# A four-layer kernel on one core: the order of its first loads, edge coefficients spread by TensorE, and buffer waits tile by tile

## The chip, the cores and the metric

The kernel runs on one core of a Trainium2 chip. A core has five engines that work side by side, each with its own stream of instructions taken strictly in order: TensorE (PE in the profile; PEld is its loading of weights), VectorE (DVE), ScalarE (ACT), GpSimd (POOL) and SyncE (SP), which here only issues transfers. ScalarE and GpSimd issue transfers too; 16 DMA engines carry all of them. The metric is device time in microseconds (us) of one launch; the median of several launches counts.

## The reference, cut to what matters

The input x has 8 sequences ("batches") of 512 rows and 512 columns, all float32. Four layers follow one another.

```python
# L0: one step of a grid operator, per batch, with finite differences
df = -(grad(A0*f, rows) + grad(A1*f, cols)) + 0.5*(grad2(B0*f, rows) + grad2(B1*f, cols) + 2 mixed terms of B2*f)
x = maximum(f + df*dt[b], 0)            # one-sided formulas on the first and last row and column
# L1: adaLN, 16-head attention with a bias and a mask, residual, then an MLP
emb = silu(sin_emb(tok)) @ W_ada + b_ada;  scale, shift = split(emb)
x = ln(x)*(1+scale) + shift
x = x + softmax(q @ k.T / sqrt(32) + bias, masked) @ v @ Wo + bo     # q, k, v = x @ Wq + bq, ...
x = x + gelu(( ln(x)*g2 + beta2 ) @ W1 + b1) @ W2 + b2
# L2: one expert per batch (Wi[e], Wo[e]), residual, layer norm
# L3: a low-rank response added with a gated strength (uses sigmoid(safety[b]))
```

In L0 the interior of the grid is the same formula everywhere; the first and the last row ("edge rows") have formulas of their own. The coefficients A and B are shared by all batches, so their combinations are formed once.

## The kernel before, in words

The program is one long list for each engine. The order on an engine is written out by hand: `pin` (`tc.keep_in_program_order`) holds an instruction at its place in the list. There are three stages.

`grid_stage` (the front) works on batch 0. It loads A and B (tiles a0, a1, b0, b1, b2), forms the coefficient sums ca, cb, cc, ce, cg on VectorE, multiplies each with f (batch 0 of x) into e, g, c, ga, gb, q, t, and lets TensorE add them up in four PSUM tiles `acc` (the profile's l_0 to l_3, one for each row that a partition holds) by multiplying with shifted identity matrices `zi`. On the way it stores the sums to DRAM as `coef_q`, `coef_e`, `coef_c`, `coef_g`, `coef_a`, `coef_b` (from GpSimd's queue, after `gate_c`), where the other batches read them again.

The edge rows of all 8 batches are computed together in a packed layout: 64 partitions stand for 4 column blocks x 2 sides x 8 batches. `fe` holds the values and `ec` the twelve rows of coefficients; `ec` is the same for all batches, so before the change `edge_in` fills it with eight broadcast loads of 8 partitions each, one after another on GpSimd's queue behind `gate_e`, a small instruction that waits for f. The result `xe` is stored to DRAM (`xed`) for the later batches, and its rows of batch 0 are copied into x (`x<-xe`, two transfers on SP, two on ACT). Then come the layer norm's statistics (`stats`), the normalisation, and `embed` (64 small matmuls, tile `pe`) with `embed_out` (tile `ada`), which give scale and shift.

`attention_stage` runs over units: batch, group of 4 heads, block of 128 rows; 128 units. Batch 0 is turned with 16 transposes (`xtr`), made into x1 by `x1_in`, and multiplied into q and k (`q_block`, `k_block`). Each unit loads two bias tiles `bt`, adds the mask on GpSimd (`add_mask`), and runs scores, softmax, transposes and values. In the same stage VectorE does the grid of the next batch in steps (`grid_early`, `grid_step`): it loads f with its neighbour rows (`gf`) and one coefficient half after another (`gq`, `x<-coef_e`, `gc`, `gg`, `ga`, `gb`), in the order that the table `GRID` gives. Step 0 is two products with gq, step 1 the product with coef_e, step 2 a difference, the product with gc, and the ghosts of the columns.

`mlp_stage` runs 16 passes: 8 of the MLP and 8 of the experts, with a seven-product form of the matmuls, whose operands are sums of quarters (`w_quads`, `b_quads`).

Tiles come from pools. A pool is opened for a stage and closed at its end, and the next pools take its memory. Transfers of SP and ACT take eight completion semaphores in turn, in program order over both; a transfer waits until the one that had its semaphore before has landed. GpSimd's have eight of their own.

In the built program the first loads stand so on SP's list (semaphore waits in brackets by their number): b1 half, a1 half, b1 half [1], a1 half [3], b0 [4], a0 [7], f [0], b2 [1], W_ada halves, Wq, Wk, Wv, Wo, bq, bk, bv, bo, then eight value loads of expert numbers, then the edge rows, mask and gf. ScalarE's list begins with ten small loads (tok, freq, b_ada, safety, eidx, ghost weights, dt, g2, beta2, b1). The first load of attention on SP (the mask `mu`) waits for all transfers, GpSimd's included, that used the memory of the closed pools.

Lines that the steps below touch: 104 to 111 (small loads), 168 (`load_w`), 175 to 178 (rows), 243 (grid matmuls), 274 to 289 (loads of the front), 386 to 393 (coef stores), 479 (xed), 492 (edge rows), 499 (stats), 546 and 543 (transposes and matmuls of attention), 588 (x1), 663 (grid sums), 973 (the softmax's first step), 1137 and 1143 (matmuls and sums of the MLP).

Of the kernel before, what the change touches and what calls it, by code (L numbers as in the profile page):

```python
# [11 lines left out]
F32 = mybir.dt.float32  # L12
# [3 lines left out]
AF = mybir.ActivationFunctionType  # L16
# [23 lines left out]
def fused_kernel(ctx: ExitStack, tc: tile.TileContext, a: dict):  # L40
# [65 lines left out]
    nc.scalar.dma_start(freq, a["c_freq"])  # L106
    bada = ep.tile([P, 2 * KC], F32, name="bada")
    nc.scalar.dma_start(bada, a["b_ada"])
    nc.scalar.dma_start(sigs, a["safety"][None, :].to_broadcast([P, NB]))
    nc.scalar.dma_start(eidx, a["eidx"][None, :])  # L110
    nc.vector.tensor_scalar(bada[:, 0:KC], bada[:, 0:KC], 1.0, None, ALU.add)
# [27 lines left out]
    nc.scalar.activation(sigs, sigs, AF.Sigmoid)  # L139
# [14 lines left out]

    def embed_out(pe):
        tc.keep_in_program_order(
            nc.vector.tensor_tensor(
                ada, pe, bada[:, :, None].to_broadcast([P, 2 * KC, NB]), ALU.add
            )
        )  # L160
# [4 lines left out]
    def load_w():  # L165
        for n in ("Wq", "Wk", "Wv", "Wo"):
            w[n] = w8(wo8, n)
            nc.sync.dma_start(w[n], a[n].rearrange("(k p) m -> p k m", p=P))
# [5 lines left out]
    def load_rows():  # L174
        nc.sync.dma_start(bqk[:, 0, :], a["bq"])
        nc.sync.dma_start(bqk[:, 1, :], a["bk"])
        nc.sync.dma_start(bvc, a["bv"].rearrange("(k p) -> p k", p=P))
        nc.sync.dma_start(bo, a["bo"][None, :].to_broadcast([P, D]))
# [3 lines left out]
        embed_out,  # L182
# [3 lines left out]
    io = ctx.enter_context(tc.tile_pool(name="io", bufs=1))  # L186
    g2 = const.tile([P, 2, KC], F32, name="g2")
    nc.scalar.dma_start(g2[:, 0, :], a["g2"])
    nc.scalar.dma_start(g2[:, 1, :], a["beta2"])
    b1 = const.tile([P, NJ], F32, name="b1")  # L190
    nc.scalar.dma_start(b1, a["b1"])
# [4 lines left out]
        g2, mhalf,  # L196
# [18 lines left out]
def grid_stage(  # L215
    tc, a, const, small, dram, x, mhalf, ident, load_wada, load_w, load_rows, embed,
    embed_out,
# [27 lines left out]
    with ExitStack() as ctx:  # L245
# [22 lines left out]
        pin(nc.gpsimd.memset(ec, 0.0))  # L268
# [7 lines left out]
        with tc.tile_pool(name="raw", bufs=1) as rp:  # L276
# [4 lines left out]
            def edge_in(i, k):  # L281
                lo, hi = max(0, W * k - 1), min(D, W * k + W + 1)
                u = slice(lo - W * k + 1, hi - W * k + 1)
                p0 = n * i
                pin(nc.gpsimd.dma_start(fe[p0 : p0 + n, :, u], a["edge_f"][:, :, lo:hi]))
                for side in range(2):
                    p1 = p0 + side * NB
                    pin(
                        nc.gpsimd.dma_start(
                            ec[p1 : p1 + NB, :, u],  # L290
                            a["edge_c"][side : side + 1, :, lo:hi].to_broadcast([NB, 12, hi - lo]),
                        )
                    )
# [9 lines left out]
            nc.scalar.dma_start(gw, a["c_ghost"].to_broadcast([P, 16]))  # L303
            nc.scalar.dma_start(dth, a["dt"][None, :].to_broadcast([P, NB]))
            load_wada()
            load_w()
# [6 lines left out]
            for i, k in enumerate(blocks):  # L313
                edge_in(i, k)
# [11 lines left out]
        wp = ctx.enter_context(tc.tile_pool(name="l0", bufs=1))  # L326
# [54 lines left out]
        for m, w, o in (  # L381
            ("q", b2, 1), ("e", ce, 1), ("c", cc, 0), ("g", cg, 1), ("a", ca, 0), ("b", cb, 0)
# [94 lines left out]
        xed = dram.tile([n, D], F32, name="xed")  # L477
        for i, k in enumerate(blocks):
            pin(nc.gpsimd.dma_start(xed[:, W * k : W * k + W], xe[n * i : n * i + n, :]))
        pe = embed(ps)  # L480
        pin(nc.vector.tensor_scalar(dth, dth, 0.5, None, ALU.mult))
        st = small.tile([P, R, 6], F32, name="ln0_st", tag="ln0_st", bufs=1)
        mv = small.tile([P, R, 2], F32, name="ln0_mv", tag="ln0_mv", bufs=1)
        for r in (0, 3, 1, 2):
            stt(x[:, r, :], acc[r], dth[:, 0:1], f[:, r, :], ALU.mult, ALU.add)
            pin(nc.scalar.activation(x[:, r, :], x[:, r, :], AF.Relu))
        for o, u, c in ((0, 3 * n, 0), (n, n, 2 * W)):
            for side, q_ in ((0, nc.sync), (1, nc.scalar)):
                p, r = side * (P - 1), side * (R - 1)
                e0 = o + side * NB  # L490
                pin(
                    q_.dma_start(
                        x[p : p + 1, r, c : c + 2 * W].rearrange("o (b w) -> o b w", w=W),
                        xe[e0 : e0 + u + 1 : u, :],
                    )
                )
# [24 lines left out]
def attention_stage(  # L521
    tc, a, small, xp, xt, x_home, x1d, grid, ident, sc1, shift, io, wo8, w, rows,
    g2, mhalf,
# [11 lines left out]
    with ExitStack() as ctx:  # L535
        wp = ctx.enter_context(tc.tile_pool(name="aw", bufs=1))
        pp = ctx.enter_context(tc.tile_pool(name="ap", bufs=2))
        ps = ctx.enter_context(tc.tile_pool(name="a_ps", bufs=1, space=PSUM))
# [508 lines left out]
        load_bias(*units[0])  # L1047
        grid_loads(1, -1)
        mask_in(0, 1)
        load_bias(*units[1])  # L1050
        for c in range(KC):
            x1_in(0, c)
        mask_out(0, 0)
# [3 lines left out]
        grid_early(0)  # L1057
# [5 lines left out]
        mask_in(0, 3)  # L1063
        grid_early(2)
# [44 lines left out]
def mlp_stage(tc, a, small, xp, io, wo8, x1d, ident, eidx, sigs, layernorm, rstd_of, phalf, wl3, g2, b1, first):  # L1109
# [19 lines left out]
    with ExitStack() as ctx:  # L1129
        wp = ctx.enter_context(tc.tile_pool(name="fw", bufs=1))  # L1130
        ap = ctx.enter_context(tc.tile_pool(name="fa", bufs=2))
        ps = ctx.enter_context(tc.tile_pool(name="f_ps", bufs=2, space=PSUM))
# [725 lines left out]
```

## Time and profile before

| | us |
|---|---|
| median of 3 runs | 2807.26 (2805.81 to 2810.29) |
| the profiled execution | 2809.32 |
| its span (first to last instruction) | 2807.5 |
| front and start, to the first softmax of unit 0 | 88.1 |
| attention, to the first matmul of the MLP | 88.1 to 1143.3 |
| MLP and experts | 1143.3 to the end |

| engine | busy us | share of the span |
|---|---|---|
| TensorE | 2729.1 | 97% |
| VectorE | 1942.0 | 69% |
| GpSimd | 1503.9 | 54% |
| ScalarE | 1002.8 | 36% |

A row of a profile names a line of the kernel, an engine, an operation and a tile (out<-in). "Busy" is the time in which the engine had an instruction. A bracket after a timeline row is the time for which the engine was idle before it and what ended that; SPq, ACTq and POOLq rows are issues of transfers, and a long issue is one that could not be handed to its queue. The chain of waits is followed back from the last instruction, at each step to what released it.

### The profile page before, as it was taken

The page shows a single profiled execution, that of the slowest core. Times are in us where ns is not written, and L with a number is a line of the kernel's source. Part 1 is how long each engine was busy: PE and PEld are TensorE (multiplying, and loading weights), DVE is VectorE, ACT ScalarE, POOL GpSimd, SP SyncE. Part 2 cuts the span into 40 slices and gives each one's busy share as a digit, 9 for nine tenths or more (in the row PEclk, how much of TensorE's full clock was granted, in tenths as well). Part 3 has the DMA queues.
Part 4 walks back from the last instruction along what each step waited for, and adds up shares of the span by engine and source line. Part 5 has one row for each costly group of instructions (what it writes and reads, how often), then busy time and mean ns, then how long its engine had stood idle before and what let it go on. Part 6 is the DMA issues. An engine that isn't in the chain of part 4 may idle for free.

```text
span 2807.5 us, 39790 instructions
## 1 busy us (share of the span) xinstructions
PE 2729.1 (97%) x14654; PEld 2011.6 (72%) x14654; DVE 1942.0 (69%) x3581; ACT 1002.8 (36%) x2133; POOL 1503.9 (54%) x1081
## 2 busy tenths in 40 slices
PE   5999999999999998999999999999999999999998
PEld 3455555555555554788888888888888888888886
DVE  6888898988888766576666756655466556556554
ACT  1466666666666666212111211211121121121221
POOL 3455555555555654466566655656456545535633
PEclk9999999999999999999999999999999999999998
DMA  9665657566666554542533444253223133143120
GB/s 300 225 204 180 235 172 241 186 223 214 194 233 191 157 160 158 181 121 49 158 124 83 109 143 124 49 169 120 73 97 125 59 137 128 42 154 113 42 75 31
DMA packets 190400, 405.62 MB, mean 144 GB/s; under 512 B 24104, under 2 KB 28784, under 8 KB 183934
## 3 DMA queue, kind: packets, MB, share of 16 engines
q1 hardware_dynamic: 185192, 391.93, 42.2%
q0 software_dynamic: 3680, 11.07, 3.2%
q8 instruction: 117, 1.92, 0.3%
q14 instruction: 77, 0.63, 0.1%
q10 hardware_dynamic: 1334, 0.07, 0.0%
HBM read 367.32 MB, written 31.50 MB: 142 GB/s over the span
## 4 chain that ended last, share of the span: by engine, by line
PE 86%; DVE 9%; ACT 2%; DMA 2%; issue 1%; SPq 0%; DVEq 0%; ACTq 0%; POOL 0%
PE y L1137 28%; PE u L1137 28%; PE tr L546 6%; PE s L543 4%; PE ctx L543 4%; PE o L543 3%; PE pv L543 3%; PE pq L543 3%; PE pk L543 2%; DVE bt L973 2%; DVE x L663 2%; DVE pt L998 1%; DMA Wo<-in_Wo 1%; ACT bt L978 1%; PE po L1137 1%; PE btr L1140 1%
## 5 line engine op out<-in xcount | busy, mean ns | idle before, releaser
L1137 PE MATMUL y<-wo,act 128*128 128x256 f32 x2560 | 578.9, 381 | 0.0
L950 POOL TENSOR_TENSOR bt<-bt,mk 128x1024 f32<-128x1024 f32 x256 | 543.2, 2142 | 64.2 <-DMA bt<-in_bias 61.2
L1137 PEld LDWEIGHTS y<-wo,act 128*128 128x128 f32 x2560 | 479.4, 190 | 82.2 <-issue 20.6
L978 ACT ACTIVATE bt<-bt,mn 128x512 f32<-128x512 f32 x512 | 365.4, 715 | 115.5 <-DVE mn L973 115.4
L546 PEld LDWEIGHTS tr<-ident,bt 128*128 128x128 f32 x2048 | 228.2, 141 | 167.7 <-issue 115.7
L1137 PE MATMUL u<-bt,wi 128*128 128x256 f32 x1440 | 330.5, 379 | 0.0
L973 DVE CUSTOM_DVE_ANT_0 bt<-s,bt 128x512 f32<-128x512 f32 x512 | 330.4, 682 | 0.0
L1143 DVE TENSOR_TENSOR act<-u,u 128x512 f32<-128x512 f32 x256 | 173.3, 686 | 209.9 <-PE u L1137 132.6
L1137 PEld LDWEIGHTS u<-bt,wi 128*128 128x128 f32 x1440 | 273.5, 190 | 37.2
L546 PE MATMUL tr<-ident,bt 128*128 128x128 f32 x2048 | 279.9, 278 | 18.8 <-DVE pt L998 7.7
L998 DVE COPY pt<-tr 128x512 f32<-128x512 f32 x256 | 175.8, 687 | 113.3 <-PE tr L546 113.0
L1137 PE MATMUL u<-tb,ws 128*128 128x256 f32 x1024 | 242.1, 379 | 0.0
L1137 PE MATMUL y<-t,s 128*128 128x256 f32 x1024 | 234.2, 380 | 0.0
L1000 ACT COPY pt<-tr 128x512 f32<-128x512 f32 x256 | 148.1, 579 | 183.1 <-PE tr L546 180.7
L1137 PEld LDWEIGHTS u<-tb,ws 128*128 128x128 f32 x1024 | 194.4, 190 | 26.5
L1146 POOL TENSOR_TENSOR t<-wo,t 128x512 f32<-128x512 f32 x64 | 104.5, 1647 | 200.5 <-PE y L1137 200.5
L1137 PEld LDWEIGHTS y<-t,s 128*128 128x128 f32 x1024 | 191.1, 190 | 24.1
L1457 ACT ACTIVATE act<-act,b 128x512 f32<-128x512 f32 x128 | 82.9, 711 | 292.4 <-DVE act L1143 292.4
L1457 ACT ACTIVATE act<-act,bi 128x512 f32<-128x512 f32 x128 | 83.8, 713 | 282.6 <-DVE act L1143 282.6
L1143 DVE TENSOR_TENSOR x<-y,x 128x512 f32<-128x512 f32 x96 | 64.5, 685 | 159.0 <-PE y L1137 105.1
L543 PE MATMUL s<-kt,qt 32*128 32x512 f32 x1024 | 171.7, 645 | 2.3 <-DVE mn L973 1.4
L1143 DVE TENSOR_TENSOR u<-u,u 128x512 f32<-128x512 f32 x192 | 131.3, 684 | 58.8 <-PE u L1137 58.8
(314 smaller groups left out, 4283.5 us busy)
## 6 DMA issues: line engine op xcount, KB each, us to landing
bt<-in_bias SPq DMA_DIRECT2D x256, 512.0 KB
wo<-in_W SPq DMA_DIRECT2D x32, 1024.0 KB
wi<-in_Wi SPq DMA_DIRECT2D x32, 1024.0 KB
wo<-in_Wo_e SPq DMA_DIRECT2D x32, 1024.0 KB
wi<-in_W SPq DMA_DIRECT2D x28, 1024.0 KB
gq<-coef_q SPq DMA_DIRECT2D x21, 512.0 KB
x1d<-x SPq DMA_DIRECT2D x8, 1024.0 KB
x<-x1d SPq DMA_DIRECT2D x8, 1024.0 KB
```

The source lines that it names most:

```text
L543: pin(nc.tensor.matmul(out, lhsT=lhsT, rhs=rhs, start=start, stop=stop))
L546: pin(nc.tensor.transpose(out, src, ident))
L663: pin(nc.vector.tensor_tensor(out, x, y, op))
L950: nc.gpsimd.tensor_tensor(bt, bt, mask[b, r][:, None, :].to_broadcast([P, 2, S]), ALU.add)
L973: nc.vector.tensor_tensor_reduce(bt[:, i, :], ss[h], bt[:, i, :], -1.0, 3.0e38, ALU.add, ALU.min, mn)
L978: nc.scalar.activation(bt[:, i, :], bt[:, i, :], AF.Exp, bias=mn, scale=-1.0, accum_out=sums[b, c, r][:, h : h + 1],)
L998: pin(nc.vector.tensor_copy(pt[:, :, r % 2, :], tr))
L1000: pin(nc.scalar.copy(pt[:, :, r % 2, :], tr))
L1137: pin(nc.tensor.matmul(out, lhsT=lhsT, rhs=rhs, start=start, stop=stop))
L1143: pin(nc.vector.tensor_tensor(out, x, y, op))
L1146: pin(nc.gpsimd.tensor_tensor(out, x, y, op))
L1457: nc.scalar.activation(acts[g][:, k, :], acts[g][:, k, :], func, bias=bi[:, j : j + 1])
```

## The change

It changes the front, the order of a few loads of attention, and how pools hand on their memory.

- Loads: safety goes first on SP, and only tok and freq stay on ScalarE. Ghost weights, dt, b_ada and eidx go on SP, behind the grids and W_ada. Wv and Wo leave the front: they are issued in attention, Wv behind the first bias and Wo behind the second. g2, beta2 and b1 go on SP, further behind (`load_late`).
- Edge coefficients: `ec8` is loaded once for 8 partitions (4 blocks x 2 sides) in four loads at the start of GpSimd's queue, and TensorE spreads each to 8 batches with a selection matrix `sel8`, in four matmuls (`pec`); ScalarE copies the four results into `ec`. Only the four loads of `fe` stay behind `gate_e`.
- The edge rows of batch 0 are issued right after rows 0 and 3 have been made, before ScalarE's Relu of rows 1 and 2. `xed` is stored from ScalarE's queue instead of GpSimd's. `coef_g` is stored before `coef_c`. The addition to b_ada stands behind the edge chain.
- `reuse_waits="tile"` on eight pools: an instruction that takes over memory of a closed pool waits for the users of the tiles that lay there, not for all of the pool. In the built program the mask's load waits for the stores of coef_a and coef_b, one of coef_q's rows, an edge row's transfer, and points on TensorE and GpSimd; gf's load for those of coef_e and coef_g and an edge row's. The first matmul of the MLP, which waited for VectorE and ScalarE, waits for ScalarE.
- Attention: `grid_early(0)` moves in front of the first mask and `q_block`, so that VectorE has the two products with gq before the first q.

```diff
+    nc.sync.dma_start(sigs, a["safety"][None, :].to_broadcast([P, NB]))
+    nc.scalar.activation(sigs, sigs, AF.Sigmoid)
     bada = ep.tile([P, 2 * KC], F32, name="bada")
-    nc.scalar.dma_start(bada, a["b_ada"])
-    nc.scalar.dma_start(sigs, a["safety"][None, :].to_broadcast([P, NB]))
-    nc.scalar.dma_start(eidx, a["eidx"][None, :])
...
     def load_rows():
+        nc.sync.dma_start(bada, a["b_ada"])
+        nc.sync.dma_start(eidx, a["eidx"][None, :])
...
-    io = ctx.enter_context(tc.tile_pool(name="io", bufs=1))
+    io = ctx.enter_context(tc.tile_pool(name="io", bufs=1, reuse_waits="tile"))
...
+    def load_late():
+        for t, v in ((g2[:, 0, :], "g2"), (g2[:, 1, :], "beta2"), (b1, "b1")):
+            tc.keep_in_program_order(nc.sync.dma_start(t, a[v]))
...
+            ec8 = rp.tile([N // NB, 12, W + 2], F32, name="ec8")
+            sel8 = rp.tile([N // NB, N // NB, NB], F32, name="sel8")
+            pin(nc.gpsimd.memset(ec8, 0.0))
...
+            for i, k in enumerate(blocks):
+                c, u = edge_cols(k)
+                pin(nc.gpsimd.dma_start(ec8[2 * i : 2 * i + 2, :, u], a["edge_c"][:, :, c]))
...
-            nc.scalar.dma_start(gw, a["c_ghost"].to_broadcast([P, 16]))
-            nc.scalar.dma_start(dth, a["dt"][None, :].to_broadcast([P, NB]))
+            nc.sync.dma_start(gw, a["c_ghost"].to_broadcast([P, 16]))
+            nc.sync.dma_start(dth, a["dt"][None, :].to_broadcast([P, NB]))
             load_wada()
-            load_w()
+            load_w("Wq", "Wk")
             load_rows()
...
             for i, k in enumerate(blocks):
-                edge_in(i, k)
+                c, u = edge_cols(k)
+                pin(nc.gpsimd.dma_start(fe[n * i : n * i + n, :, u], a["edge_f"][:, :, c]))
+
+            for i in range(4):
+                pec = ps.tile([N, 3, W + 2], F32, name=f"pec_{i}", tag="pec", bufs=2)
+                mm(
+                    pec, sel8.rearrange("q s b -> q (s b)"), ec8[:, 3 * i : 3 * i + 3, :],
+                    True, True,
+                )
+                pin(nc.scalar.copy(ec[:, 3 * i : 3 * i + 3, :], pec))
...
-            ("q", b2, 1), ("e", ce, 1), ("c", cc, 0), ("g", cg, 1), ("a", ca, 0), ("b", cb, 0)
+            ("q", b2, 1), ("e", ce, 1), ("g", cg, 1), ("c", cc, 0), ("a", ca, 0), ("b", cb, 0)
...
         for r in (0, 3, 1, 2):
             stt(x[:, r, :], acc[r], dth[:, 0:1], f[:, r, :], ALU.mult, ALU.add)
             pin(nc.scalar.activation(x[:, r, :], x[:, r, :], AF.Relu))
...
+            if r == 3:
+                edges()
+        xed = dram.tile([n, D], F32, name="xed")
+        for i, k in enumerate(blocks):
+            pin(nc.scalar.dma_start(xed[:, W * k : W * k + W], xe[n * i : n * i + n, :]))
...
-        ps = ctx.enter_context(tc.tile_pool(name="a_ps", bufs=1, space=PSUM))
+        wp = ctx.enter_context(tc.tile_pool(name="aw", bufs=1, reuse_waits="tile"))
+        pp = ctx.enter_context(tc.tile_pool(name="ap", bufs=2, reuse_waits="tile"))
+        ps = ctx.enter_context(tc.tile_pool(name="a_ps", bufs=1, space=PSUM, reuse_waits="tile"))
...
         load_bias(*units[0])
+        load_w("Wv")
         grid_loads(1, -1)
         mask_in(0, 1)
         load_bias(*units[1])
+        load_w("Wo")
         for c in range(KC):
             x1_in(0, c)
+        grid_early(0)
         mask_out(0, 0)
         pin(nc.scalar.copy(bvr, bvc[:, :, None].to_broadcast([P, KC, P])))
         add_mask(*units[0])
         drain(q_block(0, 0))
-        grid_early(0)
         grid_early(1)
         drain(k_block(0, 0, "ctx"))
         mask_out(0, 1)
         load_bias(*units[2])
         mask_in(0, 2)
         mask_in(0, 3)
+        load_late()
         grid_early(2)
```

## The prediction, made before the changed kernel was run

> **What bounds the kernel now.** I read the page first: the slices of TensorE (PE) and the shares of the chain that ended last.
>
> ```profile
> PE   5999999999999998999999999999999999999998
> ...
> PE 86%; DVE 9%; ACT 2%; DMA 2%; issue 1%; SPq 0%; DVEq 0%; ACTq 0%; POOL 0%
> ```
>
> PE carries 86% of the chain, so an edit counts only where PE has nothing to do, and the first slice (70 us, digit 5) is the one place where the page shows that. So I read the chain of waits for the first 100 us (start, duration, what).
>
> ```profile
> 26.67 34.86 DMA Wo<-in_Wo
> ...
> 61.56 3.29 DMA x<-xe
> ...
> 70.00 3.42 PE xtr L546 x16
> ```
>
> The chain runs through Wo, which lands at 61.53 and which nobody needs there: the edge rows (x<-xe) were issued behind it. The timeline of SP, of DVE and of PE shows who stands in whose way; the bracket is idle time before the row, and what ended it.
>
> ```profile
> 39.66 14.48 SPq L178 DMA_DIRECT2D bo<-in_bo  x1
> 60.72 1.38 SPq L492 DMA_DIRECT2D x<-xe  x2
> 64.93 0.34 SPq L564 DMA_DIRECT2D mu<-in_mask  x1
> 65.32 0.42 SPq L687 DMA_DIRECT2D gf<-in_x  x1
> ```
>
> ```profile
> 64.76 0.69 DVE L499 BATCH_NORM_STATS2 ln_st<-x 128x6 f32<-128x512 f32 x1 [7.64 <-DMA x<-xe]
> ...
> 76.89 0.75 DVE L617 TENSOR_SCALAR qt<-pq,bqk 128x512 f32<-128x512 f32 x1 [3.25 <-PE pq L543]
> 77.56 4.28 DVE L663 TENSOR_TENSOR gq<-gq,gf 128x1024 f32<-128x1024 f32 x2
> 81.76 3.14 DVE L663 TENSOR_TENSOR x<-x,gf 128x1024 f32<-128x1024 f32 x1
> ```
>
> ```profile
> 54.32 9.04 PE L148 MATMUL pe<-sc,wada 128*128 128x8 f32 x64
> 70.00 3.42 PE L546 MATMUL xtr<-ident,x 128*128 128x128 f32 x16 [6.64 <-DVE ada L157]
> ```
>
> SP hung on bo for 14.48 us, the edge rows came late, DVE idled 7.64 us for them, and the loads of attention (mu, gf) went out only at 65. The last view is busy time by stage (PE, PEld, DVE, ACT, POOL; then PE's clock, DMA share, GB/s).
>
> ```profile
> 6.00:12.00 6.00, 0.00 (x0) 0.00 (x0) 3.20 (x15) 3.68 (x6) 0.00 (x0) 1.00 0.70 206
> 28.00:44.00 16.00, 16.00 (x39) 7.31 (x38) 14.13 (x21) 0.17 (x1) 7.56 (x15) 1.00 1.07 215
> 44.00:62.00 18.00, 18.00 (x84) 12.23 (x82) 12.24 (x38) 2.52 (x4) 7.05 (x24) 0.93 1.03 414
> 62.00:68.00 6.00, 1.36 (x7) 1.26 (x6) 1.97 (x6) 0.00 (x0) 1.05 (x1) 0.50 0.42 116
> 72.00:88.00 16.00, 15.22 (x46) 7.18 (x45) 11.85 (x15) 5.18 (x7) 6.04 (x2) 0.97 1.03 383
> ```
>
> At 28 to 44 the DMAs are full and yet move only 215 GB/s (eight small broadcast loads of ec and four of fe run then); at 62 to 68 everything waits. From the first softmax (88.11) DVE works without a gap to 131, then PE takes over. So a shift of 88.11 passes to the end unchanged, and the sum is about that moment.
>
> **The change, part by part.**
>
> *First loads.* Before, SP's third load was issued at 5.81 and f at 10.47, because both queues take eight completion semaphores in turn and the early turns were small ScalarE loads (SP waited 4.2, 1.3 and 1.7 us for such). Now five loads go at once, and a0, f, b2 wait for tok, safety and freq, of which tok and freq landed by 6.0 and 7.4. ScalarE issued ten DMAs in the front, now two, so its table loads (1.28 us each; first at 7.67) begin earlier; the ang chain, which waited 1.52 us for the first Sin, ends about 1.2 us earlier, 9.8 for 11.02. DVE's waits in the coefficient sums (1.01, 0.38, 0.23) go, as do small gaps: from 9.8, two halves 4.6, cc 2.3, ce and cg 4.4 put e at 21.1 instead of 24.19: 3.1 us. [...] The trace decides: at 6 to 12 us the DMAs were 0.70 busy at 206 GB/s, waiting for issues; I take 3.1.
>
> *Edge coefficients by TensorE.* Eight broadcast loads become four loads of 2 partitions, 4 matmuls of N=390 and 4 copies. Costs: one pass of an l matmul (half its pair) took 0.86 us in the first 5.85 us of the block and 0.43 later, so 8 passes at 390/512 of it are 2.6 to 5.2 us; four copies at about 0.5 (hgs' kind, 512 wide, is 0.58). All before PE and ScalarE are needed, if the loads land by about 18: issued near 4, POOL's loads of ec took 8 to 9 us, so 13. Cover: PE is idle until 23.4, ScalarE until cc at 17. If it is gone, the excess falls on e one for one (rival D). The gain: qe no longer waits 1.63, and the slow stretch of 28 to 44 loses most of its small packets. Moving Wv and Wo out as well leaves about 10.6 MB of hardware loads, done by about 33, when coef stores begin.
>
> *TensorE's front.* PE worked from 26.58 to 54.32 without a gap: 27.7. From 23.5 it ends at 51.2. DVE's edge chain (t 3.1 earlier, then 0.9 + 9.05) ends at 47.8, bada's add (0.16, moved) included, so PE stays the bound. l_0 and l_3 finish about 2.6 and 1.7 before PE's end; x, Relu, and the edge rows go at 51.1 instead of 55.48 and 60.72. bo no longer blocks SP for 14.48 us: the queue ahead of it is empty by 33, and the eight value loads behind it (54.14 to 60.72, 6.6 us) end near 40. The two DMA issues on ScalarE delay Relu of x_1 and x_2 by about 1.4, in the shadow of the landing. Edge rows land at 54 to 55 (they took 3.29), stats and norm (5 us) end at 60.0. PE's embedding (9.04, same place) ends at 60.2. So xtr starts at 60.3: 9.7 earlier, bound twice over. The small loads now on SP behind the big ones (gw, dth, bada, eidx) cost 0.35 to 0.45 of issue each on a queue that is ahead of its data; gw is wanted at 32, dth at 38, bada at 47.8, eidx by SP itself, and all stand ahead of bqk, landed by 33. POOL: ec's memset (1.39) shrinks, its eight issues (0.58 each) become four, earlier; it waits there for f in any case (17.9 us).
>
> *Waits tile by tile.* mu and gf (64.93, 65.32) waited for everything in the closed pools; now mu waits for the stores of coef_a and coef_b and the last l matmul, gf for coef_e and coef_g (g is now stored before c, so it is the third of six). The stores start when q is done: 35.1. At 44 to 62 the DMAs moved 414 GB/s, so 6.3 MB take 15.2 us, to 51.5 with the first issue (0.6, and 0.6 to reach q's store), and landing is seen some 1.7 later (bt's bytes had passed at 76.0 by the rates, its first user began at 77.78): 53 to 54. [...] the trace's 414 held for 18 us, so I take it. gf also waits for an edge row's semaphore, its small pieces for those of the xed stores, now on ScalarE's queue at 53.5. gf: 55.0 for 65.32, 10.3 earlier. xed off POOL (2.03 of issue) saves nothing: POOL was free.
>
> *Wv and Wo between the coefficients.* After gf the queue was the limit: gf 1.57 MB, gq 1.05, bt 1.05, then coef_e, 4.25 MB with mu. By the rates above these had passed at 78.4 and coef_e was usable near 80. Wv (1.05 MB) now stands ahead of coef_e: 2.7 us at 383 GB/s. coef_e: 80 - 10.3 + 2.7 = 72.4. Wo comes ahead of coef_g only (another 2.7), used 8 us later than e's successors; with two biases coef_a lands at about 85 and is wanted at 87.7. load_late's three loads (g2, beta2, b1; 12 KB, one issue of 0.34 each) go in front of coef_a on SP: 1 us of issue, inside the 3 us that coef_a has in hand; their users run 1 ms later.
>
> *grid_early(0) before q_block.* gq's two products (1.2 each uncontended; 3.1 for the one beside POOL's mask add) fill the 3.25 us in which DVE waited for pq. gq lands near 65.3, products end 67.7, qt 68.5. Then DVE waits for coef_e: 72.4; e0, w0, c0, ghosts 1.2 x 3 + 1.1 (before, e0 took 3.14 beside POOL): softmax at 77.3 instead of 88.11. **Sum of the front: 10.8.** Scores (xtr 60.3, x1, pq, pk 3.45 each, kt) are ready by 73.
>
> *Turn to the MLP.* At 1142.48 PE waited 0.88 us for DVE's last x (o_3) before u: the pool wait. Now u waits for ScalarE only. DVE's following sums were just in time (ws and tb done by 1146.1, wanted at 1146.4), so 0.5 to 0.85: 0.6. Elsewhere in the MLP only loads' waits move.
>
> Total 11.4. The profiled execution took 2809.3 (span 2807.5 and 1.8 around it); the median of the runs is 2807.26, 2.1 below. 2807.3 - 11.4 = **2796**.
>
> Unknown costs: 8 passes of pec 0 or, if late, one for one; coef stores 51 to 57; [...] Wv and Wo 2.1 to 5.4 on the path. Together 5.5 to 14.5 of gain.
>
> **The rivals.**
> B. *The loads run faster still.* With the slow stretch gone, stores end at 51, gf goes at 52.5 and DVE hardly waits for coef_e. 13.7 + 0.6: 2793. For: 215 against 414 GB/s. Against: PE's embedding holds xtr at 60.3 anyway.
> C. *The stores stay late.* coef_b took 13.9 us and landed at 63.8; if they end near 59, gf goes at 60: 10.8 falls to 5.8, time 2801. For: coef_a and coef_b still wait for coef_q's semaphore. If they end as before (64), coef_e lands at 82 and 1.3 + 0.6 are left, 2805: no change.
> D. *Slower: PE stuck at pec.* PE's and ScalarE's streams are in order, so l<-e and cc stand behind the ec8 loads. Behind l the rest takes 27.2 + 9.1 to xtr; xtr is later than 72.9 (70.0 and the 2.9 saved behind it) if e starts after 36.5, that is if ec8 lands after about 33. Landing at 40: xtr 79.4, time 2814. Against: the longest landing of POOL's queue in the trace is 15.6 us (coef_g), so 20.
> E. *Nothing arrives.* The waits differ but the coefficients' bytes bound DVE as before; this is C's end point.
>
> **How the numbers follow.** Likeliest (my sum) 0.55, 2796 with 2793 to 2799; B 0.21; C 0.17; its end point with no change 0.04; D 0.03. A measurement here tells about 0.2%, 5.6 us. Leaving out D, the end point and the outer edges of B and C gives 2790.5 to 2801.5. Faster 0.93, same 0.04, slower 0.03.
>
> **What would show it.** Right: pec near 13 us, l<-e near 23.5, PE's l block ending near 51, xtr near 60, gf issued near 55, first softmax near 77 with a DVE wait for coef_e of about 4 us before it, no gap between o and u. Wrong: l<-e behind a wait for ec8; gf still after 60 with stores as the releaser; a wait at coef_g or coef_a, which would return part of the gain; or a DVE gap after 88 us that was not there before.

## The result, and the profile after

The changed kernel took 2797.38 us (median of 8 runs, 2795.12 to 2800.91) against 2808.82 us for the kernel before on the same chip (8 runs): 11.4 us less, a ratio of 0.9961 (95% interval 0.9951 to 0.9972). The forecast was 2796, or 11.4 less. A second set of runs gave 2798.51 beside 2808.41 (0.9960, 0.9947 to 0.9974). Runs of either kernel scatter over some 5 us (2805.81 to 2810.29 before, 2795.12 to 2800.91 after); TensorE's clock, below, has a part in it.

First the slices of PE and the chain by engine. The first slice has digit 7 instead of 5, and nothing else stands out.

```profile
PE   7999999999999998999999999999999999999998
...
PE 87%; DVE 9%; ACT 2%; DMA 1%; issue 1%; SPq 0%; ACTq 0%; DVEq 0%; POOL 0%
```

The chain of waits for the first 80 us (start, duration, what; L numbers are now lines of the changed kernel). Wo and the landing of the edge rows have gone from it; the stores of xed and the load of coef_e have come in.

```profile
54.23 5.21 DMA xed<-xe
...
62.39 9.95 DMA x<-coef_e
72.36 1.23 DVE x L687
```

The timelines of SP, DVE and PE, for the rows shown of before. bo (256 KB in both) blocks SP for 1.30 us instead of 14.48; the edge rows go at 49.29 instead of 60.72, mu at 52.82 instead of 64.93, gf at 53.34 instead of 65.32.

```profile
27.82 1.30 SPq L184 DMA_DIRECT2D bo<-in_bo  x1
49.29 1.97 SPq L507 DMA_DIRECT2D x<-xe  x2
52.82 0.34 SPq L588 DMA_DIRECT2D mu<-in_mask  x1
53.34 0.55 SPq L711 DMA_DIRECT2D gf<-in_x  x1
...
58.91 0.22 SPq L715 DMA_DIRECT2D gf<-in_x  x1
```

What SP waited for at 48 to 66 us (us, times, longest): a small piece of gf (L715) for a store of xed (the next piece waited 0.3 more), and mu (L588) for an edge row.

```profile
SPq L715 <- DMA xed<-xe: 2.9, 1, 2.9
SPq L588 <- DMA x<-xe: 1.3, 1, 1.3
```

```profile
52.67 0.69 DVE L523 BATCH_NORM_STATS2 ln_st<-x 128x6 f32<-128x512 f32 x1 [1.49 <-ACT x L515]
...
63.85 2.50 DVE L687 TENSOR_TENSOR gq<-gq,gf 128x1024 f32<-128x1024 f32 x2 [0.61 <-DMA gq<-coef_q]
67.65 0.75 DVE L641 TENSOR_SCALAR qt<-pq,bqk 128x512 f32<-128x512 f32 x1 [1.31 <-PE pq L567]
72.36 1.23 DVE L687 TENSOR_TENSOR x<-x,gf 128x1024 f32<-128x1024 f32 x1 [3.96 <-DMA x<-coef_e]
...
76.80 0.69 DVE L997 CUSTOM_DVE_ANT_0 bt<-s,bt 128x512 f32<-128x512 f32 x1
```

```profile
13.36 5.43 PE L251 MATMUL pec<-ec,sel 8*64 8x390 f32 x8 [13.36 <-DMA ec<-in_edge_c]
23.00 5.88 PE L251 MATMUL l<-e,zi 128*128 128x512 f32 x8 [4.22 <-DVE e L245]
...
50.22 9.51 PE L145 MATMUL pe<-sc,wada 128*128 128x8 f32 x64
59.59 3.65 PE L570 MATMUL xtr<-ident,x 128*128 128x128 f32 x16
```

DVE stood 7.64 us for the edge rows and stands 1.49 for a Relu now; the two gq products lie ahead of qt, which waits 1.31 for pq instead of 3.25; the one long wait left is 3.96 for coef_e. The first softmax starts at 76.80 instead of 88.11: 11.3 us earlier. By stage (PE, PEld, DVE, ACT, POOL; PE's clock, DMA share, GB/s), the DMAs work from 6 us on, the stretch of 28 to 44 moves 300 GB/s for 215, and at 62 to 68 PE works the whole time, at a clock of 0.75.

```profile
6.00:12.00 6.00, 0.00 (x0) 0.00 (x0) 5.33 (x15) 1.94 (x4) 1.27 (x4) 1.00 1.05 383
28.00:44.00 16.00, 16.00 (x45) 7.59 (x44) 15.37 (x35) 0.17 (x1) 8.45 (x22) 1.00 0.82 300
...
62.00:68.00 6.00, 6.00 (x16) 3.29 (x15) 3.60 (x4) 2.20 (x4) 0.71 (x1) 0.75 0.96 339
```

At the turn to the MLP, u starts with the end of o (1114.73 + 13.90 is 1128.63, u at 1128.46); before, it waited 0.88 us for DVE. Here are the first u and a y some 56 us later, before and then after.

```profile
1143.34 3.69 PE L1137 MATMUL u<-hT,w 128*128 128x256 f32 x16 [0.88 <-DVE x L655]
...
1198.67 7.07 PE L1137 MATMUL y<-t,s 128*128 128x256 f32 x32
```

```profile
1128.46 3.62 PE L1164 MATMUL u<-hT,w 128*128 128x256 f32 x16
...
1184.23 7.07 PE L1164 MATMUL y<-t,s 128*128 128x256 f32 x32
```

The two profiles are 14.88 us apart at u and 14.44 at y: half of the 0.88 is given back at once, since u now runs ahead of DVE's sums for its next products (its weight loads wait 0.22 us for tb and 0.38 for hT). Of the 14 profiles here, the 12 without the gap at u all lose 0.4 to 0.5 us in this stretch against the two with it (before and e1), so the turn is worth 0.4 us.

The profiled executions differ by 13.9 us (2809.32 and 2795.37), more than the medians. The rest is TensorE's clock: near 1085 us it was at half in the profile of before and full in that of after. Here is busy time at 1080 to 1092, the clock third from the end; before first.

```profile
1080.00:1092.00 12.00, 10.42 (x62) 5.21 (x61) 5.31 (x15) 6.01 (x14) 10.10 (x5) 0.72 0.39 146
```

```profile
1080.00:1092.00 12.00, 10.64 (x80) 5.92 (x79) 6.71 (x19) 8.15 (x21) 8.54 (x4) 1.00 0.44 136
```

That cost the profiled execution of before 3.1 us: the two are 10.7 us apart at a softmax at 1063.98 (1053.26 after) and 13.8 at the last o (1128.57 and 1114.73). So 11.3 at the first softmax, 0.9 at the turn and 3.1 of clock make 15.3, of which 1.4 were given back: about 0.4 in small steps before u, 0.4 right behind it, and the rest in the last 20 us, which was not followed up.

### The profile page after: what moved, and what is told of

It reads as the page before. It is cut to its first block, busy times and chain, and to the rows that moved or that the text cites. A ratio compares the mean times of both kernels' runs of the same rounds, so it can differ in the third digit from the quotient of the medians.

```text
span 2793.6 us, 39799 instructions
## 1 busy us (share of the span) xinstructions
PE 2731.8 (98%) x14662; PEld 2012.1 (72%) x14662; DVE 1940.4 (69%) x3581; ACT 1004.3 (36%) x2137; POOL 1499.5 (54%) x1074
## 4 chain that ended last, share of the span: by engine, by line
PE 87%; DVE 9%; ACT 2%; DMA 1%; issue 1%; SPq 0%; ACTq 0%; DVEq 0%; POOL 0%
PE y L1164 28%; PE u L1164 28%; PE tr L570 7%; PE s L567 4%; PE ctx L567 4%; PE o L567 3%; PE pv L567 3%; PE pq L567 3%; PE pk L567 2%; DVE bt L997 2%; DVE x L687 2%; DVE pt L1022 1%; ACT bt L1002 1%; PE po L1164 1%; PE btr L1167 1%; PE l L251 1%
## 5 line engine op out<-in xcount | busy, mean ns | idle before, releaser
L1164 PEld LDWEIGHTS y<-wo,act 128*128 128x128 f32 x2560 | 479.3, 190 | 82.4 <-issue 20.5
```

The source lines that it names most:

```text
L1164: pin(nc.tensor.matmul(out, lhsT=lhsT, rhs=rhs, start=start, stop=stop))
```

## The experiments

The theory: one shift of the first softmax by 11 us, made of parts that stand in series, and nearly 1 us at the turn. The rivals: one part alone is the gain; or it is a matter of the clock. Medians of 5 to 13 runs scatter by 1 to 2 us, and the clock goes with it (the runs of the changed kernel at 2795.1 to 2796.1 us show a mean clock of 0.994, those at 2798.6 to 2800.9 one of 0.991 to 0.993), so a part is judged by where the first softmax starts in its profile, and the time stands beside it. The two profiles of the changed kernel differ by 0.2 us there, so steps of that size say nothing. The last column is from the first softmax to the first u. What differs in it is mostly TensorE's clock near 1080 us: 1051.4 to 1051.7 where it did not fall to half there (changed, e8, e6), 1054.2 to 1055.5 where it was at half for 6.8 us. In e10 and e11 that stretch is 3.4 us long, in e12 there are two of 3.4 us, and e9 and e10 lost 4.6 and 1.5 us more at an earlier place, by 150 us.

| kernel | median us | 95% interval of the ratio to before | first softmax | to first u |
|---|---|---|---|---|
| before | 2808.82 | | 88.11 | 1055.2 |
| changed | 2797.38 | 0.9951 to 0.9972 | 76.80 | 1051.7 |
| changed, again (e8) | 2798.51 | 0.9947 to 0.9974 | 76.58 | 1051.4 |
| e1 no tile waits | 2799.76 | 0.9959 to 0.9981 | 78.00 | 1055.4 |
| e2 tile waits alone, on before | 2807.38 | 0.9987 to 1.0004 | 87.67 | 1055.0 |
| e3 Wv, Wo in front | 2798.37 | 0.9951 to 0.9978 | 77.80 | 1054.2 |
| e4 products late | 2799.82 | 0.9949 to 0.9977 | 77.67 | 1055.5 |
| e5 broadcast loads | 2799.85 | 0.9958 to 0.9982 | 78.65 | 1054.2 |
| e6 pec's loads late | 2806.45 | 0.9989 to 1.0006 | 86.38 | 1051.6 |
| e7 small loads first | 2802.84 | 0.9970 to 0.9988 | 79.42 | 1055.1 |
| e9 Wv behind coef_e | 2795.33 | 0.9938 to 0.9965 | 76.52 | 1059.5 |
| e10 xed on POOL | 2794.89 | 0.9936 to 0.9963 | 75.49 | 1054.1 |
| e11 both of these | 2794.66 | 0.9941 to 0.9968 | 74.11 | 1053.5 |
| e12 e3 and e5 together | 2808.75 | 0.9988 to 1.0005 | 87.88 | 1052.3 |

**e1, the changed kernel without tile waits**, on all eight pools:

```diff
-tc.tile_pool(name="io", bufs=1, reuse_waits="tile")
+tc.tile_pool(name="io", bufs=1)
```

> The changed kernel, with reuse_waits="tile" taken off all eight pools; every instruction stays in its place. My theory (one shift of the first softmax, made of parts in series, plus the turn to the MLP): mu and gf wait again for the last user of everything in the closed pools, and that is now the landing of the xed stores at about 59.4 us. So gf goes at about 60 instead of 53.3; its small pieces, which waited for xed in any case, then follow at once, so gq goes at about 63.5 instead of 59.7, coef_e is usable near 76.3 instead of 72.4 and the first softmax starts near 81 instead of 76.8. The gap of about 0.9 us between o and u is back. Time about 2802.5 (2801 to 2804) against 2797.4. Rival 1, the tile waits are the whole gain: 2808. Rival 2, they only move waits about: 2797.4.

The softmax moved by 1.2 us, not 4. What SP waited for at 48 to 66 us (us, times, longest):

```profile
SPq L704 <- DMA gf<-in_x: 2.6, 1, 2.6
SPq L588 <- DMA x<-xe: 2.2, 1, 2.2
SPq L588 <- DMA xed<-xe: 1.7, 4, 1.1
```

mu went at 55.45, as the stores of xed landed then and not at 59.4 (gf was not yet on its way), and the small pieces of gf, behind it, waited no more. Then SP was ahead of its data again and stood 2.6 us for a semaphore of gf: the delay of the issue was mostly swallowed there. The 0.88 us ahead of u came back (`[0.88 <-DVE x L679]`). The tile waits are worth 1.2 us in the front and, by the rows behind u, 0.4 at the turn, once all else is changed.

**e2, the kernel before with tile waits alone.** The same edit, on before.

> The kernel before, with reuse_waits="tile" on the eight pools and nothing else. My theory: mu and gf stand on SP behind the edge rows, whose issue ends at 62.1, so gf goes near 62.7 instead of 65.3; but DVE still waits for the edge rows until 64.8, xtr stays at 70 and qt at 77, and DVE's sums, which end at 88, hardly wait for loads behind that. The first softmax moves by 0 to 2 us and the turn gives 0.9. Time 2806 to 2808 against 2808.8, most likely 2807. Rival 1, the tile waits are the whole gain: 2797.4. Rival 2, parts add up without being in series: the 2.6 us of gf and the 0.9 of the turn, 2805.3.

As expected: 1.3 us by the medians (2807.38, with 2808.66 for before beside it), inside the scatter. The first softmax moved by 0.4, since the edge rows stand ahead of everything:

```profile
64.31 0.69 DVE L499 BATCH_NORM_STATS2 ln_st<-x 128x6 f32<-128x512 f32 x1 [7.37 <-DMA x<-xe]
```

The rival that the tile waits are the whole gain has fallen from both sides.

**e3, Wv and Wo in the front again.**

```diff
-            load_w("Wq", "Wk")
+            load_w("Wq", "Wk", "Wv", "Wo")
...
-        load_w("Wv")
-        load_w("Wo")
```

> The changed kernel, with Wv and Wo loaded in the front again, behind Wq and Wk; nothing else. My theory: 2.1 MB more stand in the queue ahead of bqk, bo and beside the coefficient stores, about 5.5 us at 383 GB/s. The stores end that much later, gf goes near 58 instead of 53.3; on the other side Wv no longer stands ahead of coef_e (2.7 us). coef_e is usable near 74.5, the first softmax near 79. bo blocks SP longer, but ends ahead of the edge rows at 49.3, as the slow broadcast loads are gone. Time about 2799.5 (2797 to 2802). Rival 1, Wv and Wo in front were the main cause: the edge rows are late again, 2805 to 2809. Rival 2, the stores aren't slowed, and Wv's place ahead of coef_e is a pure loss: 2794.7.

1.0 us at the softmax. bo still issued in 1.22 us and the edge rows at 49.84. coef_e was there 0.7 us earlier than in the changed kernel, as Wv no longer stood ahead of it; but its product now met GpSimd's mask add (GpSimd is busy for 1.51 us of 72 to 76 here, in the changed kernel not at all) and took 2.89 us instead of 1.23, and that is more than the 1.0 us.

```profile
71.70 2.89 DVE L687 TENSOR_TENSOR x<-x,gf 128x1024 f32<-128x1024 f32 x1 [2.96 <-DMA x<-coef_e]
```

The late Wo, which headed the chain of before, is no cause by itself once ec's eight broadcast loads are gone.

**e4, the two gq products behind the first q again.**

```diff
-        grid_early(0)
         mask_out(0, 0)
...
         drain(q_block(0, 0))
+        grid_early(0)
         grid_early(1)
```

> The changed kernel, with grid_early(0) (the two gq products) back behind the first q block; nothing else. My theory now: the products (2.5 us) go behind qt at 68.4 and end at 70.9, ahead of coef_e at 72.4, so they are hidden by the wait for coef_e, which shrinks from 3.96 to about 1.5 us: no change, 2797.4. Rival, DVE's amount of work sets the moment of the first softmax: 2.5 us later, 2799.9. In between if the products run beside POOL's mask add (from 67.3): up to 1.5 us later.

0.9 us: between the two. The wait for coef_e does cover them, but at 68 us they run beside GpSimd's mask add (GpSimd is busy for all of 68 to 72) and take 5.10 us instead of 2.50, which ends 1 us after coef_e was there in the changed kernel (72.36).

```profile
68.22 5.10 DVE L687 TENSOR_TENSOR gq<-gq,gf 128x1024 f32<-128x1024 f32 x2
73.25 1.22 DVE L687 TENSOR_TENSOR x<-x,gf 128x1024 f32<-128x1024 f32 x1
```

**e5, the edge coefficients by eight broadcast loads.**

```diff
-                pin(nc.gpsimd.dma_start(ec8[2 * i : 2 * i + 2, :, u], a["edge_c"][:, :, c]))
...
+                for side in range(2):
+                    p1 = n * i + side * NB
+                    pin(nc.gpsimd.dma_start(ec[p1 : p1 + NB, :, u],
+                        a["edge_c"][side : side + 1, :, c].to_broadcast([NB, 12, c.stop - c.start])))
...
-                mm(pec, sel8.rearrange("q s b -> q (s b)"), ec8[:, 3 * i : 3 * i + 3, :], True, True)
-                pin(nc.scalar.copy(ec[:, 3 * i : 3 * i + 3, :], pec))
```

> The changed kernel, with the edge coefficients ec loaded as before, by eight broadcast loads on POOL's queue behind gate_e, without the four matmuls, the copies and ec8. My theory: PE and ScalarE don't notice it. The broadcast loads fill the queues with small packets again while the coefficient stores go: the stores end 1 to 4 us later, gf goes at 55 to 57 instead of 53.3 and the first softmax starts at 77.5 to 79.5 instead of 76.8. DVE's edge sums wait up to 2 us for ec, hidden behind PE. Time about 1.5 us above the changed kernel (0.5 to 3). Rival 1, the slow packets were what held the front: 5 us or more. Rival 2, nothing: the same time, since the queue has room when the stores begin.

1.9 us, as expected. With the DMAs at a share of 1.06 from 28 to 44 us (0.82 in the changed kernel), the store of coef_a had to wait 3.68 us for coef_q's landing (0.41 there). gf itself went at 54.27, not at 55 to 57; its last small piece went at 61.13 instead of 59.45.

```profile
42.34 0.54 POOL L394 DMA_DIRECT2D coef_a<-ca  x1 [3.68 <-DMA coef_q<-b]
```

**e6, the price of case D:** the four loads of ec8 behind `gate_e`.

```diff
+            pin(nc.gpsimd.tensor_tensor(gate, f[:, 0, 0:1], f[:, 0, 0:1], ALU.add))
             for i, k in enumerate(blocks):
                 c, u = edge_cols(k)
                 pin(nc.gpsimd.dma_start(ec8[2 * i : 2 * i + 2, :, u], a["edge_c"][:, :, c]))
...
-            pin(nc.gpsimd.tensor_tensor(gate, f[:, 0, 0:1], f[:, 0, 0:1], ALU.add))
```

> The changed kernel, with the four loads of ec8 moved from the front of POOL's queue to behind gate_e (f's landing, 17 to 18 us); all else as it is. It measures the price of case D of the prediction, PE and ScalarE standing in order behind pec. My theory: ec8 lands near 27, pec takes 5.4 us, l<-e starts near 32.5 instead of 23.0, and cc's scaling on ScalarE, which stands behind the copies, is late by more than 10 us, so DVE's c and q come later too. xtr goes at 69 instead of 59.6, gf at 59 to 60, the first softmax at 84 to 86: 8 us slower than the changed kernel (6 to 10). Rival, the excess is hidden because coef_e is what DVE waits for: 0 to 4 us.

9.6 us at the softmax and 7.9 by the medians (2806.45 and e8's 2798.51): nearly the whole gain. PE's list stands for the loads, ScalarE's list stands behind PE, and DVE, whose e began at 19.73, stands for a scaling on ScalarE that has nothing to do with edges. PE, then DVE:

```profile
27.00 5.43 PE L251 MATMUL pec<-ec,sel 8*64 8x390 f32 x8 [27.00 <-DMA ec<-in_edge_c]
32.36 6.04 PE L251 MATMUL l<-e,zi 128*128 128x512 f32 x8
```

```profile
34.78 2.29 DVE L245 TENSOR_TENSOR c<-cc,f 128x2048 f32<-128x2048 f32 x1 [10.56 <-ACT cc L339]
```

xtr came at 68.98, 9.4 later than in the changed kernel, as l<-e came 9.4 later: one for one, as case D had it.

**e7, the small loads on ScalarE in their old order.**

```diff
-    nc.sync.dma_start(sigs, a["safety"][None, :].to_broadcast([P, NB]))
+    nc.scalar.dma_start(bada, a["b_ada"])
+    nc.scalar.dma_start(sigs, a["safety"][None, :].to_broadcast([P, NB]))
+    nc.scalar.dma_start(eidx, a["eidx"][None, :])
...
-            nc.sync.dma_start(gw, a["c_ghost"].to_broadcast([P, 16]))
-            nc.sync.dma_start(dth, a["dt"][None, :].to_broadcast([P, NB]))
+            nc.scalar.dma_start(gw, a["c_ghost"].to_broadcast([P, 16]))
+            nc.scalar.dma_start(dth, a["dt"][None, :].to_broadcast([P, NB]))
```

g2, beta2 and b1 likewise, and the sigmoid back behind the Silu.

> The changed kernel, with the small loads (b_ada, safety, eidx, c_ghost, dt, g2, beta2, b1) issued by ScalarE in their old order again; nothing else. My theory: SP's third load waits for a turn behind small loads again, ScalarE's tables come later, e starts at 23 instead of 20.6 and l<-e at 25.5 instead of 23.0; this passes to xtr (62) and to the coefficient stores, so the first softmax starts near 79 instead of 76.8, and the time is about 2.3 us above the changed kernel (1.5 to 3). [...]

e at 23.22, l<-e at 25.66, xtr at 62.28, softmax at 79.42: 2.6 us, passed through undiminished. What held VectorE is not a large load: from 11.96 on it forms the coefficient sums without a wait for any. It began them 3.4 us later than in the changed kernel (8.55), because freq landed 2.0 us later (8.31 for 6.29 in the row that needs it) and then the first Sin was late on ScalarE (1.52 us of waiting, as in the kernel before), whose table loads stand behind its issues of small loads: in the kernel before the first began at 7.67, behind eight of them, in the changed kernel at 1.69, behind two.

```profile
8.31 0.36 DVE L116 TENSOR_SCALAR ang<-tf,freq 128x8 f32<-128x8 f32 x2 [1.62 <-DMA freq<-in_c_freq]
...
11.66 0.17 DVE L134 TENSOR_TENSOR ang<-ang,neg 128x16 f32<-128x16 f32 x1 [1.52 <-ACT sc L130]
...
11.96 1.22 DVE L247 TENSOR_TENSOR ca<-b,a 128x1024 f32<-128x1024 f32 x1
```

The median is 4.3 above that of e8 (2798.51), which is more. The half clock near 1080 us is in this profile and not in that of e8; whether it makes up the rest, this does not settle.

**e8, the changed kernel again.**

> The changed kernel once more, unaltered, beside the three others on the same chip. Its runs so far fall into two groups, four near 2795.4 us at a mean clock of 0.994 and four at 2798.6 to 2800.9 at 0.991 to 0.993; of 19 runs of the kernel before, 17 lie at 2807.4 to 2810.2 and two near 2805. All profiles but that of the changed kernel show a stretch of some 7 us near 1080 us in which TensorE's clock is at half. If that stretch comes at random with one chance for every kernel, most runs lie near 2800 now, and the gain like for like is 8 to 10 us rather than 11.4; if the change makes it rarer, about half lie near 2795.4 again.

Two of five runs lie at 2792.9 and 2794.9, three at 2798.5 to 2799.7. The profiled one (2794.92) has full clock at 1072 to 1092. So the answer is the second: in both sets together 6 of 13 runs of the changed kernel lie below 2796.2, against 6 of 77 runs of before that lie below 2806. Why the stretch is rarer after the change was not tried.

**e9, e10, e11, is there more?** Wv behind coef_e and coef_c; the stores of xed on GpSimd's queue as soon as xe is there; both.

```diff
-        load_w("Wv")
         grid_loads(1, -1)
+        load_w("Wv")
```

> The changed kernel, with Wv's load moved behind those of coef_e and coef_c (it stood ahead of both); nothing else. My theory: coef_e is usable 2.3 to 2.7 us earlier (1 MB at about 383 GB/s), near 69.9 instead of 72.3; DVE's wait of 3.9 us for it shrinks to about 1.4, the first softmax starts near 74.3 instead of 76.7; Wv lands near 72.5, just as PE comes to pv. About 2.4 us faster than the changed kernel. Rival, the wait moves on: PE stands at pv for Wv, or DVE for coef_g or coef_a, and 0 to 1 us are left.

```diff
+            pin(nc.gpsimd.dma_start(xed[:, W * k : W * k + W], xe[n * i : n * i + n, :]))
         pe = embed(ps)
...
-            pin(nc.scalar.dma_start(xed[:, W * k : W * k + W], xe[n * i : n * i + n, :]))
```

> The changed kernel, with the four xed stores on POOL's queue, issued as soon as xe is ready (near 47.5 us), instead of on ScalarE's behind the Relus; nothing else. The prediction said that xed off POOL saves nothing. My theory: it costs; the small pieces of gf no longer wait on SP for the landing of xed (2.9 us), gq goes at 56.5 instead of 59.7 and coef_e is usable near 71.1 instead of 72.3 (the queue, not the issue, sets the rest): first softmax 75.5, 1.2 us faster. Rival 1: the stores land behind coef_b's megabytes on POOL's queue, near 54, and nothing changes in gf. Rival 2: the whole 3 us of issue come back: 73.7.

> The changed kernel with both: Wv behind coef_e and coef_c, and the xed stores on POOL's queue. My theory: the two gains add up until DVE's wait for coef_e is gone: coef_e usable near 68.7, first softmax near 73.1 instead of 76.7, where the first scores (72.9) become the limit. About 3.6 us faster than the changed kernel. Rival: xtr, pq and pk on PE, or the second coefficients, hold the front, and no more than the better of the two alone is left.

e9: coef_e was usable 1.95 us earlier (70.41), but its product then ran beside the mask add (GpSimd busy for 3.98 us of 68 to 72; 2.90 us instead of 1.23), the softmax gained no more than the 0.3 us by which profiles differ, and PE stood for Wv. The rival is right: the wait moved on. The profiled execution is also the slowest of the five by 7 us (2803.23; the others 2794.29 to 2796.10): from 73.5 us on, in that stand and behind it, the clock was at half for 6.8 us.

```profile
74.44 16.91 PE L567 MATMUL pv<-Wv,x 128*128 128x512 f32 x32 [2.18 <-DMA Wv<-in_Wv]
```

e10: gf's last small piece at 56.48 instead of 59.45, coef_e at 71.05, softmax at 75.49: the 1.2 us of the theory, give or take 0.1. e11: no wait for coef_e is left, the softmax is at 74.11, 2.7 us earlier. But PE comes to pv at 72.86, as in the changed kernel (72.90), and is busy with it to 86.7. So of the 2.7, 1.65 are left at the softmax of the second unit (94.13 for 95.78), and 0.8 at the first u (1127.62 for 1128.46), with 3.4 us of half clock near 1072 that the changed kernel's profile doesn't have. The medians of the three lie 2 to 3 us below the changed kernel's, with intervals that overlap its own: that they are faster isn't shown. What it shows is the next bound: PE from xtr on.

**e12, e3 and e5 undone together.** Alone they cost 1.0 and 1.9 us; all the parts taken back alone (e1, e3, e4, e5, e7) add up to 7.5 of 11.3. (Not taken back at all were the edge rows' place ahead of two Relus, coef_g ahead of coef_c, and the place of the addition to b_ada; no other pair was tried.)

> The changed kernel with two parts undone at once, each of which cost little alone: ec by the eight broadcast loads behind gate_e (alone: first softmax at 78.7 instead of 76.7) and Wv and Wo loaded in the front (alone: 77.8). If parts simply add, the first softmax starts near 79.7, 3 us late. My theory: together they fill the queues until the coefficient stores start, bo's issue blocks SP as in the kernel before (14.5 us there, 3.7 and 1.2 in the two alone), the edge rows go out late, after 52 instead of 49.3, and the stores end near 58 or later: xtr at 62 to 66, first softmax at 81 to 84, 5 to 7 us late, time about 2803 to 2806. Rival 1, they only add: 3 us late. Rival 2, one covers the other: 2 us.

11.1 us at the softmax: the whole gain of the front, 4 us more than the theory's upper end, and the time of before. SP, then DVE, then PE:

```profile
26.09 12.63 SPq L179 DMA_DIRECT2D bada<-in_b_ada  x1
...
45.68 10.12 SPq L184 DMA_DIRECT2D bo<-in_bo  x1
63.18 1.39 SPq L496 DMA_DIRECT2D x<-xe  x2
```

```profile
59.72 0.17 DVE L154 TENSOR_SCALAR bada<-bada 128x4 f32<-128x4 f32 x1 [13.24 <-DMA bada<-in_b_ada]
```

```profile
70.00 4.40 PE L559 MATMUL xtr<-ident,x 128*128 128x128 f32 x16 [11.08 <-DVE x L524]
```

b_ada's 4 KB stand on SP behind Wo. With ec's broadcast loads and the 2 MB of Wv and Wo the DMAs work without a break from 24 to 58 us, through the start of the coefficient stores (those of the changed kernel stand still from 33.6 to 36.0, and its first store is issued at 35.16), and b_ada lands only at 59.7; DVE's list stands for an addition of 0.17 us, and x, the edge rows and the norm behind it. xtr starts at 70.00, exactly as before the change, for another reason: there the edge rows stood behind bo, here behind b_ada. With one of the two parts in place b_ada is there in time (its addition waits for nothing, at 47.2 us in e3 and 46.6 in e5); it takes both undone to lose it.

## Why the prediction was right

Step by step, with what the runs show:

- *First loads*: e came at 20.57 (forecast 21.1, before 24.19), and e7 gives 2.6 us for this step alone, against 3.1. The sum split it into 1.2 us of the ang chain and the rest in waits for A and B. By the rows the ang chain has most of it: the coefficient sums began at 8.55 instead of the 9.8 of the sum (before 11.02), and in e7 they wait for no load at all. Of the waits of SP that the sum put down to small loads, the longest was for SP's own first load (`SPq L274 <- DMA b<-in_B: 4.2, 1, 4.2`); the small loads' part in it was that six of the eight turns had gone to them. Who issues the small loads, and when, is worth those 2.6 us here: work of ScalarE that others wait for stands behind its issues (its first table load at 7.67 before, at 1.69 after).
- *Edge coefficients by TensorE*: ec8 at 13.36 (13), 5.43 us on PE (2.6 to 5.2; just above), four copies of 0.48. cc's scaling stood behind the copies, from 15.85 to 19.20, and ended 3.9 us before its user came at 24.98, so it cost nothing. The price of a lost cover is e6.
- *TensorE's front*: l ended at 50.2 (51.2), xtr at 59.59 (60.3), with norm and embedding ending within 0.5 us of one another. The delay of ScalarE's Relu was foreseen at 1.4, in the shadow of the edge rows' landing; DVE stood 1.49 for it (`ACT x L515` above), so the Relu and not the landing came last.
- *Stores and gf*: coef_b landed 12.7 us after its issue at 40.34, at 53.0 (53 to 54), and the DMAs moved 399 GB/s from 36 to 51 us, so the trace's 414 was a good rate to take. But this landing isn't what mu and gf waited for. An edge row released mu (1.3 us, above) at 52.82, 0.2 us before coef_b was there; in e11 mu went at 51.51, 1.75 us before it. So gf's start at 53.34, 1.7 earlier than forecast, comes from edge rows that were issued 1.8 earlier than forecast; that the path through the stores gave nearly the same moment is luck. Then the small pieces of gf waited for xed, 2.9 and 0.3 us, until 59.45. The sum had named that wait and given it no length; it is the missing term. 1.7 early and 3.2 late would put coef_e at 73.9; it came at 72.36, forecast 72.4. Half of the difference is Wv's smaller price (next point), the other half was not traced: luck again. "xed off POOL saves nothing" is right as a gain and wrong as a balance: on ScalarE's queue it costs about 1.2 us (e10).
- *Wv*: 2.7 us ahead of coef_e; e9 has 1.95, and nothing of it was to be had, since the product then meets the mask add and PE needs Wv at the same time.
- *grid_early(0)*: ended 66.3 (67.7), worth 0.9 us (e4), through avoiding the mask add rather than through filling the wait.
- *First softmax*: 76.80 (77.3); 11.3 us instead of 10.8.
- *Turn*: the gap of 0.88 is gone and 0.44 of it is left behind it; the sum took 0.6 net, since DVE's sums were "just in time". They were not quite.
- *Rivals*: B, C and the end point would have shown in gf at 52.5 or 60; gf's start lay near B's, the end of its issue (59.45) near C's. D's mechanism is real (e6: ec8 at 27.0 costs 9.6 us, one for one from there on, so the gain is gone near 29 rather than the 33 of the working), its condition missed by 15 us.

One thing in the sum was not foreseen and helped it: the medians differ by 11.4 partly because the half clock near 1080 us is rarer after the change (neither profile of the changed kernel has it, that of before has 6.8 us). From the rows, the profiled pair without it differs by 13.9 - 3.1 = 10.8. So the mechanism, one shift of the first softmax that passes to the end, was right; that the forecast hit the median to 1.4 us is partly luck.

## What to carry to other kernels

Parts that look small when taken back one by one can be substitutes for each other: price them in pairs before calling any of them useless, above all where they fill the same queue (e3 1.0 us, e5 1.9, both 11.1). A small load that someone waits for belongs ahead of the large ones, even when today's queue is empty in time (4 KB of b_ada behind Wo: no wait in e3, 13.24 us in e12). And when an engine's list gets a new instruction that waits for a load, ask who stands behind it on that engine, and who stands for those: in e6 the price was paid three engines on. Where an instruction waits for several things, ask the trace which of them ends last: the program named the stores, and an edge row decided.

## What the hardware did that was not expected

TensorE's clock was at 0.50 for 6.8 to 20.5 us in the front of each of the fourteen profiles, and the stretch moved with the embedding, not with time: it began 3.7 to 5.4 us after the first pe matmul (54.32 and 59.4 before; 50.22 and 54.8 after; 59.74 and 64.4 in e6; 53.44 and 58.6 in e7). Before the change PE idled through nearly half of it (busy 7.01 of 13.65 us); after it, pe's second half, xtr and the first 2 us of pq run in it, and pq takes 4.58 us instead of the 3.60 of e3, where the clock was back. The embedding is 64 matmuls of 8 columns; before the change PE had worked without a gap from 26.58 us up to it.

The lengths come in steps of 3.41 us. Here are three stretches of the kernel before (the clock is third from the end): half, full, half.

```profile
59.40:73.05 13.65, 7.01 (x35) 6.94 (x35) 4.89 (x12) 0.78 (x1) 1.05 (x1) 0.50 0.74 257
73.05:103.77 30.72, 27.84 (x83) 12.06 (x81) 27.23 (x33) 10.49 (x20) 10.41 (x5) 1.00 0.75 262
103.77:107.18 3.41, 3.08 (x4) 1.17 (x4) 3.37 (x6) 1.06 (x1) 0.53 (x2) 0.50 0.98 324
```

13.65, 30.72 and 3.41 us are 4, 9 and 1 times 3.41. In all fourteen profiles, at 50 to 160 us and at 1060 to 1140, every stretch at half clock is 1, 2, 3, 4 or 6 times 3.41 us long. Each begins a whole number of such steps after the first of its profile: 13, 20, 27 and 300 before, 18 and 25 after, and so in the others as closely as stretches of 1 to 4 us show it. Where the first begins differs from one execution to the next (54.8 and 54.4 us in the two profiles of the changed kernel). What sets the clock, and why the stretch near 1080 us is in some profiles and not in others, these runs don't show.

A product of 1.22 us on VectorE took 2.62 (e11) to 3.15 us (before) beside GpSimd's mask add. Five of the changes tried here moved a product into that overlap ahead of the first softmax (e3 2.89, e9 2.90, e11 2.62, e12 2.84 us; e4 5.10 for two), and the change itself took two out of it (3.15 and 3.14 us before), which is why shifts of a microsecond did not pass on as they were: 1.95 us at coef_e became 0.3 at the softmax in e9.
